# A two-layer transformer block with cross attention on one core: eight PSUM banks divided five and three, one maximum per head

## The chip, the cores and the metric

The kernel runs on one core of a Trainium2 chip. The metric is the device time of one execution in microseconds (us), from runs on the chip. In this kernel TensorE (PE) multiplies and writes to eight PSUM banks (tiles of 128 partitions x 512 fp32 values); VectorE (DVE) and ScalarE (ACT) read them; GpSimd (POOL) works on tiles in SBUF; SyncE (SP) issues most DMAs.

## The reference

The input is x (4 x 512 x 320) and a context (4 x 1601 x 192), fp32. Two layers of the same form follow one another; each adds three parts to x:

```python
h1 = _ln(x, n1_g, n1_b)
x = _attn(h1, h1, q1, k1, v1, o1_w, o1_b, heads) + x        # self attention, 512 keys
h2 = _ln(x, n2_g, n2_b)
x = _attn(h2, context, q2, k2, v2, o2_w, o2_b, heads) + x   # cross attention, 1601 keys
h3 = _ln(x, n3_g, n3_b)
a, g = jnp.split(h3 @ ff_w1 + ff_b1, 2, axis=-1)
x = a * jax.nn.gelu(g, approximate=False) @ ff_w2 + ff_b2 + x
```

Attention has 20 heads of 16 columns and a softmax over all keys.

## The kernel before

**Units and rounds.** Attention is cut into units: one batch and one group of four heads (5 groups), so 20 units of self and 20 of cross attention per layer, then four feed-forward units. main (L1157) runs a unit in rounds, one for each chunk of 128 keys: 4 rounds for self attention, 13 for cross attention, 680 in all. In a round each of the four heads gets its scores (score, L1161): keys on the partitions, 512 queries along the bank, three matmul passes of 32 rows: two for the products of a value split in a high and a low part, and one that subtracts the row maximum (nrows). ACT takes the exponential (L1178). The round after, values (L1185) multiplies the four exponentials with the values (tile av, L1192), ACT copies the result (vo, L1208) and POOL adds it up (L1209).

**Maxima.** The maximum of each query's scores must be known before its unit starts. It is found by computing the scores once more, with queries on the partitions (tile sps, L968), and reducing along the keys on DVE (L985). max_pairs (L945) prepares this work for the unit that is next: for each 128 queries and 512 keys a pair of heads (2, 3) and a pair (0, 1). The 65 keys that are left over in cross attention are done for all queries at once (L996, L1008). give (L1438) hands main one pair of each kind per round, as long as there are some; what is left runs in extra rounds of its own (L1233, L1242), in which start["both"] is set.

**How a round is ordered.** The heads use different rows of the PE array, so passes of different heads run side by side. round_of (L1140) makes all tiles of a round first, lays their passes out in slots by the rows they use, issues slot after slot, and only then issues the readers (exponentials and reductions):

```python
made = [f() for f in products]
...
for at in sorted(slots):
    for p in slots[at]:
        p()
for _, _, then in made:
    then()
```

The products are scores 0 and 1, pair (2, 3), scores 2 and 3, pair (0, 1). So the slots are: scores 0, 1 with maxima 2, 3 (two slots); then scores 2, 3 start where the maxima end, and maxima 0, 1 start in the fourth slot, after scores 0 and 1.

**Side steps.** Between rounds, steps (L429) runs work for later units by costs and due times: projections (qkps, qps, kps), values (vps), the output projection (ops), norms. Queries and keys that have been projected go through DMAs to their places. Each engine executes its instructions in the order in which the program issues them.

**The banks.** Two pools hold the eight PSUM banks. ps_st (L97) has four single banks: scores, av, and the side steps' tiles (step_bank, L369). ps_m (L98) has two tiles of two banks: a pair of maxima, reduced by one DVE instruction, fills one. quarter_banks (L871), for the keys and values of the context (L826, L910), takes two single banks and one pair: ACT copies the singles (L835, L918), DVE the pair with one instruction (L836, L919). The feed-forward part (banks, L1324) takes two single banks and one pair for two chunks. A tile that is allocated waits until the readers of an earlier tile in its bank are done; the wait stands on the first matmul that writes the bank.

Of the kernel before, what the change touches and what calls it, by code (L numbers as in the profile page):

```python
# [9 lines left out]
F32 = mybir.dt.float32  # L10
# [3 lines left out]
ALU = mybir.AluOpType  # L14
AX = mybir.AxisListType
PSUM = bass.MemoryType.PSUM

B, N, D = 4, 512, 320
S2, CTX = 1601, 192
H, DH = 20, 16  # L20
# [3 lines left out]
P = 128  # L24
NQ = N // P
G, HG = 5, 4
# [15 lines left out]
HALF = QT // 2  # L42
# [24 lines left out]
def kernel(ctx: ExitStack, tc: tile.TileContext, x, context, ws, out):  # L67
# [18 lines left out]
    nc = tc.nc  # L86
# [7 lines left out]
    shared = ctx.enter_context(tc.tile_pool(name="shared", bufs=1))  # L94
    prs = ctx.enter_context(tc.tile_pool(name="prs", bufs=9))
    dram = ctx.enter_context(tc.tile_pool(name="dram", bufs=1, space=bass.MemoryType.DRAM))
    ps_st = ctx.enter_context(tc.tile_pool(name="ps_st", bufs=4, space=PSUM))  # L97
    ps_m = ctx.enter_context(tc.tile_pool(name="ps_m", bufs=2, space=PSUM))  # L98
    ctx.enter_context(tc.manual_schedule())


# [267 lines left out]
    def step_bank(shape, name):  # L369

        if start["on"] and start["both"]:
            return ps_m.tile([P, 2, 512], F32, tag="m", name=name)[:, 0]
        return ps_st.tile(shape, F32, tag="st", name=name)

    def warm(n):
# [312 lines left out]
    def add_proj(u):  # L688
# [129 lines left out]
        def keys_of_context():  # L818

            pss, singles, pair = quarter_banks("kps")  # L820
            for k in range(KB):
                for a, ps in enumerate(pss):
                    rows = slice(a * SLOT, (a + 1) * SLOT)
                    for i in range(2):
                        w = HALF + 32
                        nc.tensor.matmul(  # L826
                            ps[i * GD : (i + 1) * GD, :w],
                            lhsT=wk_q[rows, k, u.g * GD : (u.g + 1) * GD],
                            rhs=first.kvT[rows, k, i * HALF : i * HALF + w],
                            start=(k == 0),  # L830
                            stop=(k == KB - 1),
                        )
            low, high = (room[n].rearrange("p (a w) -> p a w", a=4) for n in ("low", "high"))
            for i, ps in enumerate(singles):
                nc.scalar.copy(low[:, 3 * i, :], ps[:, : HALF + 32])  # L835
            nc.vector.tensor_copy(low[:, 1:3, :], pair[:, :, : HALF + 32])  # L836
            split(room["low"], room["high"])

            parts = high, low

            def full(i):
                to = u.kT[:, : 4 * QT].rearrange("p (a w) -> p a w", a=4)
                return [
                    (to[h::2, :, i * HALF : (i + 1) * HALF], t[i * GD : (i + 1) * GD, :, :HALF]) for h, t in enumerate(parts)
                ]

            def ends():
                to = u.kT[:, 4 * QT :].rearrange("p (a w) -> p a w", a=4)
                return [(to[h::2], t[GD:, :, HALF:]) for h, t in enumerate(parts)]

            move("k", lambda: full(0), free, GAP + 1)
            move("k", lambda: full(1), free)
            move("k", ends, free)
            first.made["kv"] += 1
# [15 lines left out]

    def quarter_banks(name):  # L871

        both = ps_m.tile([P, 2, 512], F32, tag="m", name=name)
        singles = [ps_st.tile([P, 512], F32, tag="st", name=name) for _ in range(2)]
        return [singles[0], both[:, 0], both[:, 1], singles[1]], singles, both

    def add_values(u):

# [23 lines left out]
        def values_of_context(i, s):  # L902

            h0, h1 = PARTS[i]
            w = (h1 - h0) * DH
            pss, singles, both = quarter_banks("vps")
            for k in range(KB):
                for a, ps in enumerate(pss):
                    rows = slice(a * SLOT, (a + 1) * SLOT)
                    nc.tensor.matmul(  # L910
                        ps[:, :w],
                        lhsT=u.kvT[rows, k, s * P : (s + 1) * P],
                        rhs=wv_q[rows, k, h0 * DH : h1 * DH],
                        start=(k == 0),
                        stop=(k == KB - 1),
                    )
            for a, ps in enumerate(singles):
                nc.scalar.copy(vals[:, 4 * s + 3 * a, h0:h1, 0:DH], ps[:, :w].rearrange("p (h d) -> p h d", d=DH))  # L918
            nc.vector.tensor_copy(  # L919
                vals[:, 4 * s + 1 : 4 * s + 3, h0:h1, 0:DH],  # L920
                both[:, :, :w].rearrange("p a (h d) -> p a h d", d=DH),
            )
            u.vmade[i] += 4

        for i, g in enumerate((0, 2)):
# [19 lines left out]
    def max_pairs(u):  # L945
# [8 lines left out]
        def banks(heads):  # L954


            if start["both"] and heads[0] == 0:
                pss = [ps_st.tile([P, 512], F32, tag="st", name="sps") for _ in heads]
                return pss, [ps.rearrange("p (o w) -> p o w", o=1) for ps in pss]
            ps = ps_m.tile([P, 2, 512], F32, tag="m", name="sps")  # L960
            return [ps[:, i] for i in range(2)], [ps]

        def full_two(heads, t, s):
            pss, parts = banks(heads)

            def product(e):
                for j, ps in zip(heads, pss):
# [11 lines left out]
                to = u.pm[:, t, :, s]  # L979

            def reduce():
                n = 2 // len(parts)
                for i, part in enumerate(parts):
                    j = heads[0] + i
                    nc.vector.tensor_reduce(to[:, j : j + n], part, AX.X, ALU.max, negate=(ns == 1))  # L985

            return heads, [lambda e=e: product(e) for e in range(2)], reduce

        def rest_two(heads):
            pss, parts = banks(heads)  # L990
            w = rest + rest % 2

            def product(t):
# [8 lines left out]
                        )  # L1002

            def reduce():
                n = 2 // len(parts)
                for i, part in enumerate(parts):
                    j = heads[0] + i
                    nc.vector.tensor_reduce(  # L1008
                        u.pm[:, :, j : j + n, full].rearrange("p t j -> p j t"),
                        part[:, :, : NQ * w].rearrange("p j (t w) -> p j t w", w=w)[:, :, :, :rest],  # L1010
                        AX.X,
                        ALU.max,
                    )

            return heads, [lambda t=t: (product(t), product(t + 1)) for t in range(0, NQ, 2)], reduce
# [141 lines left out]
    def main(u, give, nxt):  # L1157
# [55 lines left out]
        for c in range(u.nch):  # L1213
            extra = []
            if last:

                both = ps_m.tile([P, 2, N], F32, tag="m", name="st")
                round_of([lambda j=j: score(c, j, both[:, j % 2] if j > 1 else None) for j in range(HG)])
                tick()
            else:  # L1220
                products = []
# [48 lines left out]
    def ff_main(u, give, nxt):  # L1270
# [50 lines left out]
            nc.scalar.activation(gl, pss[1], AF.Gelu, bias=b1[:, NHC + c : NHC + c + 1])  # L1321
            nc.vector.scalar_tensor_tensor(hid[c], pss[0], b1[:, c : c + 1], gl, ALU.add, ALU.mult)  # L1322

        def banks():  # L1324
            gates = ps_m.tile([P, 2, 512], F32, tag="m", name="fps")
            return [[ps_st.tile([P, 512], F32, tag="st", name="fps"), gates[:, e]] for e in range(2)]


        pss = None
        for c in range(0, NHC, 2):  # L1330
            ahead = pss is not None
            if not ahead:
                beside(True, 2)
                pss = banks()

            for e in range(2):
                if e or ahead:
# [3 lines left out]
            if not ahead:  # L1341
                rests(c, these, False)
                if c + 2 < NHC:
                    pss = banks()
                    rests(c + 2, pss, True)
            for e in range(2):
                gate(c + e, these[e])
# [221 lines left out]
```

## Time and profile before

| what | value |
| --- | --- |
| median of 3 runs | 3118.38 us (3117.67 to 3122.93) |
| the profiled execution | 3113.44 us, of which its span 3111.7 us |
| granted TensorE clock | 0.993 of full speed |
| attention of layer 0, from 390 us to 1300 us | PE busy 882.18 us of 910.00, DVE 708.91, ACT 711.12 |
| feed-forward of layer 0, from 1300 us to 1590 us | PE busy 287.45 us of 290.00, DVE 77.71, ACT 42.02 |

In the profile, a line number (L968) is a line of the kernel before. A group of instructions shows the tile written and the tiles read, the count, its busy time with the mean of one in ns, and the time that its engine stood idle before it with what ended that. PE shows matmuls, PEld the loading of their weights. A timeline row is the start, the time taken, the engine, the line and the operation. A matmul of fp32 operands leaves two records, one of the split operands one.

### The profile page before, as it was taken

What the parts mean: (1) busy time and instruction counts of PE and PEld (TensorE: products, weight loads), DVE (VectorE), ACT (ScalarE), POOL (GpSimd) and SP (SyncE); (2) the same over time, 40 slices, a digit from 0 to 9 for tenths busy, and PEclk for the clock granted to TensorE, in tenths of its full rate; (3) what the DMA queues carried; (4) which work ended last, traced back from release to release, by engine and by line L of the source; (5) the groups of instructions that cost most, each with busy time, mean ns of one, the idle gap of its engine ahead of it and who ended that gap; (6) DMA issues with size and microseconds to landing.
All of it is one profiled execution on the core that took longest, in us unless ns stands there. A gap on an engine that the chain in (4) does not pass through costs nothing.

```text
span 3111.7 us, 81138 instructions
## 1 busy us (share of the span) xinstructions
PE 2997.5 (96%) x34290; PEld 1601.3 (51%) x34290; DVE 2115.3 (68%) x2834; ACT 1961.0 (63%) x3909; POOL 1129.4 (36%) x1213
## 2 busy tenths in 40 slices
PE   7999899999999999999999998999999999999999
PEld 4555455455455555355555554554545545544555
DVE  5887877877878788522258778778787787774221
ACT  3776567777877778611137765678778778784110
POOL 3434234444444543311114442445444444431000
PEclk8999999999999999999999999999999999999999
DMA  3433122221221221200114332211221122102000
GB/s 96 112 87 104 48 66 62 67 51 40 62 56 36 62 53 27 82 6 0 31 31 105 88 83 53 58 46 45 53 55 41 42 58 47 44 16 80 9 13 13
DMA packets 188189, 165.54 MB, mean 53 GB/s; under 512 B 67748, under 2 KB 152880, under 8 KB 187824
## 3 DMA queue, kind: packets, MB, share of 16 engines
q1 hardware_dynamic: 187240, 159.28, 20.1%
q8 instruction: 270, 4.42, 0.6%
q14 instruction: 95, 0.78, 0.1%
q10 hardware_dynamic: 360, 0.53, 0.1%
q0 software_dynamic: 224, 0.53, 0.1%
HBM read 43.53 MB, written 28.90 MB: 23 GB/s over the span
## 4 chain that ended last, share of the span: by engine, by line
PE 78%; DVE 14%; ACT 5%; issue 1%; POOL 1%; SPq 0%; DMA 0%; ACTq 0%; POOLq 0%; DVEq 0%
PE st L1168 23%; PE av L1192 18%; PE fps L1298 9%; DVE pm L985 6%; PE yps L1352 6%; PE qkps L763 4%; ACT pr L1178 4%; PE kps L826 3%; PE sps L968 3%; PE vps L910 3%; PE ops L1102 3%; PE fps L1311 2%; DVE nmax L985 2%; PE qps L802 2%; PE vps L892 2%
## 5 line engine op out<-in xcount | busy, mean ns | idle before, releaser
L1178 ACT ACTIVATE pr<-st 128x512 f32<-128x512 f32 (+1 forms) x2720 | 1405.4, 603 | 340.7 <-PE st L1168 277.2
L985 DVE TENSOR_REDUCE pm<-sps 128x2 f32<-128x1024 f32 (+1 forms) x982 | 1129.1, 1192 | 124.0 <-PE sps L968 107.0
L1209 POOL TENSOR_TENSOR o<-o,vo 128x512 f32<-128x512 f32 x576 | 741.7, 1288 | 1271.5 <-ACT vo L1208 1265.1
L1168 PE MATMUL st<-q,kT 32*128 32x512 f32 (+1 forms) x5120 | 951.5, 436 | 19.8 <-DVE x L1109 8.2
L968 PE MATMUL sps<-kT,q 32*128 32x512 f32 x4800 | 840.2, 437 | 39.3 <-DVE pm L985 19.5
L1192 PE MATMUL av<-pr,vals 128*32 128x512 f32 (+1 forms) x5440 | 736.8, 608 | 32.3 <-ACT pr L1178 25.5
L1168 PEld LDWEIGHTS st<-q,kT 32*128 32x128 f32 (+1 forms) x5120 | 468.2, 180 | 495.3 <-ACT pr L1178 277.1
L1168 PE MATMUL st<-nrows,ones 32*128 32x512 f32 (+1 forms) x2720 | 631.1, 395 | 0.1
L985 DVE TENSOR_REDUCE nmax<-sps 128x2 f32<-128x1024 f32 (+1 forms) x338 | 377.5, 1160 | 110.0 <-PE sps L968 107.8
L968 PEld LDWEIGHTS sps<-kT,q 32*128 32x128 f32 x4800 | 363.9, 183 | 91.5 <-DVE pm L985 52.4
L1208 ACT COPY vo<-av 128x512 f32<-128x512 f32 x576 | 348.6, 605 | 31.5 <-PE av L1192 23.7
L1168 PEld LDWEIGHTS st<-nrows,ones 32*128 32x128 f32 (+1 forms) x2720 | 329.0, 180 | 32.2 <-issue 0.6
L1321 ACT ACTIVATE gl<-fps,b 128x512 f32<-128x512 f32 x80 | 50.7, 684 | 385.2 <-PE fps L1311 275.4
L1298 PE MATMUL fps<-hT,w 128*128 128x512 f32 x640 | 283.7, 597 | 1.1 <-DVE hid L1322 1.1
L1192 PEld LDWEIGHTS av<-pr,vals 128*32 128x32 f32 (+1 forms) x5440 | 110.7, 108 | 290.4 <-ACT pr L1178 279.9
L1322 DVE SCALAR_TENSOR_TENSOR hid<-fps,b,gl 128x512 f32<-128x512 f32 x80 | 56.4, 746 | 255.2 <-ACT gl L1321 255.2
L1298 PEld LDWEIGHTS fps<-hT,w 128*128 128x128 f32 x640 | 119.2, 190 | 150.8 <-issue 144.9
L1352 PE MATMUL yps<-w,hid 128*128 128x320 f32 x640 | 175.8, 434 | 0.4 <-ACT hT L535 0.4
L1352 PEld LDWEIGHTS yps<-w,hid 128*128 128x128 f32 x640 | 120.5, 190 | 56.0 <-issue 6.6
L1102 PEld LDWEIGHTS ops<-wo,aT 112*32 112x32 f32 (+1 forms) x3072 | 97.4, 110 | 61.3 <-issue 29.7
L763 PE MATMUL qkps<-hT,wqk 112*128 112x256 f32 (+1 forms) x480 | 125.1, 404 | 0.9 <-DVE hid L1322 0.9
L1102 PE MATMUL ops<-wo,aT 112*32 112x160 f32 (+1 forms) x3072 | 124.1, 300 | 0.9 <-DVE pm L985 0.5
(92 smaller groups left out, 2409.8 us busy)
## 6 DMA issues: line engine op xcount, KB each, us to landing
kT<-stages SPq DMA_DIRECT2D x160, 192.0 KB
oway<-o SPq DMA_DIRECT2D x80, 256.0 KB
q<-high SPq DMA_DIRECT2D x160, 64.0 KB
q<-low SPq DMA_DIRECT2D x160, 64.0 KB
kT<-high SPq DMA_DIRECT2D x60, 128.0 KB
q<-low SPq DMA_DIRECT2D x58, 128.0 KB
kT<-low SPq DMA_DIRECT2D x58, 128.0 KB
q<-high SPq DMA_DIRECT2D x56, 128.0 KB
```

The lines of the kernel that those rows point to most:

```text
L763: nc.tensor.matmul(ps[:, :w], lhsT=wqk[:n, k, u.g].rearrange("p i d -> p (i d)"), rhs=first.hT[:n, k, at : at + w], start=(k == 0), stop=( ...
L826: nc.tensor.matmul(ps[i * GD : (i + 1) * GD, :w], lhsT=wk_q[rows, k, u.g * GD : (u.g + 1) * GD], rhs=first.kvT[rows, k, i * HALF : i * HAL ...
L968: nc.tensor.matmul(ps, lhsT=u.q[j * SLOT : (j + 1) * SLOT, e, t * P : (t + 1) * P], rhs=u.kT[j * SLOT : (j + 1) * SLOT, u.k0 + s * 512 : u ...
L985: nc.vector.tensor_reduce(to[:, j : j + n], part, AX.X, ALU.max, negate=(ns == 1))
L1102: nc.tensor.matmul(ps[f : f + m, : D // 2], lhsT=aT[:n, k, t * P + f : t * P + f + m], rhs=wo[:n, k, cols], start=(k == 0), stop=(k == 2),)
L1168: nc.tensor.matmul(st[:r, :], lhsT=ones[rows, :r] if e == 2 else u.keys(rows, c), rhs=u.rows[rows, :] if e == 2 else u.q[rows, e, :], star ...
L1178: nc.scalar.activation(p[:r], st[:r], AF.Exp)
L1192: nc.tensor.matmul(ps[j * SLOT : (j + 1) * SLOT, :], lhsT=columns_of[:r, head : head + SLOT], rhs=pr.pop((c, j))[:r, :], start=True, stop= ...
L1208: nc.scalar.copy(vo, ps)
L1209: nc.gpsimd.tensor_tensor(u.o, u.o, vo, ALU.add)
L1298: nc.tensor.matmul(ps, lhsT=w1[:, k, i * FF + c * P : i * FF + (c + 1) * P], rhs=u.hT[:, k, :], start=ahead and k == 0, stop=not ahead and ...
L1352: nc.tensor.matmul(ps[:, :D], lhsT=hid[c][:, t * P : (t + 1) * P], rhs=w2[:, c, :], start=(c == 0), stop=(c == NHC - 1),)
```

## The change

ps_st gets five banks, and ps_m three single banks instead of two pairs. A pair of maxima takes two tiles of ps_m and is reduced by two DVE instructions, one per head; the pair that DVE copied in the context's keys and values becomes two tiles and two copies. A side step in an extra round takes one bank of ps_m instead of a pair. In the last unit of a layer, scores 2 and 3 take a bank each. The feed-forward part takes two banks of each pool for the first two chunks and, for the two chunks that follow at once, three of ps_st and one of ps_m.

```diff
@@ -94,8 +94,8 @@
     shared = ctx.enter_context(tc.tile_pool(name="shared", bufs=1))
     prs = ctx.enter_context(tc.tile_pool(name="prs", bufs=9))
     dram = ctx.enter_context(tc.tile_pool(name="dram", bufs=1, space=bass.MemoryType.DRAM))
-    ps_st = ctx.enter_context(tc.tile_pool(name="ps_st", bufs=4, space=PSUM))
-    ps_m = ctx.enter_context(tc.tile_pool(name="ps_m", bufs=2, space=PSUM))
+    ps_st = ctx.enter_context(tc.tile_pool(name="ps_st", bufs=5, space=PSUM))
+    ps_m = ctx.enter_context(tc.tile_pool(name="ps_m", bufs=3, space=PSUM))
     ctx.enter_context(tc.manual_schedule())
 
 
@@ -369,7 +369,7 @@
     def step_bank(shape, name):
 
         if start["on"] and start["both"]:
-            return ps_m.tile([P, 2, 512], F32, tag="m", name=name)[:, 0]
+            return ps_m.tile([P, 512], F32, tag="m", name=name)
         return ps_st.tile(shape, F32, tag="st", name=name)
 
     def warm(n):
@@ -833,7 +833,8 @@
             low, high = (room[n].rearrange("p (a w) -> p a w", a=4) for n in ("low", "high"))
             for i, ps in enumerate(singles):
                 nc.scalar.copy(low[:, 3 * i, :], ps[:, : HALF + 32])
-            nc.vector.tensor_copy(low[:, 1:3, :], pair[:, :, : HALF + 32])
+            for i, ps in enumerate(pair):
+                nc.vector.tensor_copy(low[:, 1 + i, :], ps[:, : HALF + 32])
             split(room["low"], room["high"])
 
             parts = high, low
@@ -870,9 +871,8 @@
 
     def quarter_banks(name):
 
-        both = ps_m.tile([P, 2, 512], F32, tag="m", name=name)
-        singles = [ps_st.tile([P, 512], F32, tag="st", name=name) for _ in range(2)]
-        return [singles[0], both[:, 0], both[:, 1], singles[1]], singles, both
+        scored, maxed = ([pool.tile([P, 512], F32, tag=tag, name=name) for _ in range(2)] for pool, tag in ((ps_st, "st"), (ps_m, "m")))
+        return [scored[0], maxed[0], maxed[1], scored[1]], scored, maxed
 
     def add_values(u):
 
@@ -916,10 +916,10 @@
                     )
             for a, ps in enumerate(singles):
                 nc.scalar.copy(vals[:, 4 * s + 3 * a, h0:h1, 0:DH], ps[:, :w].rearrange("p (h d) -> p h d", d=DH))
-            nc.vector.tensor_copy(
-                vals[:, 4 * s + 1 : 4 * s + 3, h0:h1, 0:DH],
-                both[:, :, :w].rearrange("p a (h d) -> p a h d", d=DH),
-            )
+            for a, ps in enumerate(both):
+                nc.vector.tensor_copy(
+                    vals[:, 4 * s + 1 + a, h0:h1, 0:DH], ps[:, :w].rearrange("p (h d) -> p h d", d=DH),
+                )
             u.vmade[i] += 4
 
         for i, g in enumerate((0, 2)):
@@ -954,14 +954,11 @@
         def banks(heads):
 
 
-            if start["both"] and heads[0] == 0:
-                pss = [ps_st.tile([P, 512], F32, tag="st", name="sps") for _ in heads]
-                return pss, [ps.rearrange("p (o w) -> p o w", o=1) for ps in pss]
-            ps = ps_m.tile([P, 2, 512], F32, tag="m", name="sps")
-            return [ps[:, i] for i in range(2)], [ps]
+            pool, tag = (ps_st, "st") if start["both"] and heads[0] == 0 else (ps_m, "m")
+            return [pool.tile([P, 512], F32, tag=tag, name="sps") for _ in heads]
 
         def full_two(heads, t, s):
-            pss, parts = banks(heads)
+            pss = banks(heads)
 
             def product(e):
                 for j, ps in zip(heads, pss):
@@ -979,15 +976,13 @@
                 to = u.pm[:, t, :, s]
 
             def reduce():
-                n = 2 // len(parts)
-                for i, part in enumerate(parts):
-                    j = heads[0] + i
-                    nc.vector.tensor_reduce(to[:, j : j + n], part, AX.X, ALU.max, negate=(ns == 1))
+                for j, ps in zip(heads, pss):
+                    nc.vector.tensor_reduce(to[:, j : j + 1], ps, AX.X, ALU.max, negate=(ns == 1))
 
             return heads, [lambda e=e: product(e) for e in range(2)], reduce
 
         def rest_two(heads):
-            pss, parts = banks(heads)
+            pss = banks(heads)
             w = rest + rest % 2
 
             def product(t):
@@ -1002,14 +997,9 @@
                         )
 
             def reduce():
-                n = 2 // len(parts)
-                for i, part in enumerate(parts):
-                    j = heads[0] + i
+                for j, ps in zip(heads, pss):
                     nc.vector.tensor_reduce(
-                        u.pm[:, :, j : j + n, full].rearrange("p t j -> p j t"),
-                        part[:, :, : NQ * w].rearrange("p j (t w) -> p j t w", w=w)[:, :, :, :rest],
-                        AX.X,
-                        ALU.max,
+                        u.pm[:, :, j, full], ps[:, : NQ * w].rearrange("p (t w) -> p t w", w=w)[:, :, :rest], AX.X, ALU.max,
                     )
 
             return heads, [lambda t=t: (product(t), product(t + 1)) for t in range(0, NQ, 2)], reduce
@@ -1214,8 +1204,9 @@
             extra = []
             if last:
 
-                both = ps_m.tile([P, 2, N], F32, tag="m", name="st")
-                round_of([lambda j=j: score(c, j, both[:, j % 2] if j > 1 else None) for j in range(HG)])
+                round_of([
+                    lambda j=j: score(c, j, ps_m.tile([P, N], F32, tag="m", name="st") if j > 1 else None) for j in range(HG)
+                ])
                 tick()
             else:
                 products = []
@@ -1321,9 +1312,12 @@
             nc.scalar.activation(gl, pss[1], AF.Gelu, bias=b1[:, NHC + c : NHC + c + 1])
             nc.vector.scalar_tensor_tensor(hid[c], pss[0], b1[:, c : c + 1], gl, ALU.add, ALU.mult)
 
-        def banks():
-            gates = ps_m.tile([P, 2, 512], F32, tag="m", name="fps")
-            return [[ps_st.tile([P, 512], F32, tag="st", name="fps"), gates[:, e]] for e in range(2)]
+        def banks(spare):
+            def bank(e):
+                pool, tag = (ps_m, "m") if e else (ps_st, "st")
+                return pool.tile([P, 512], F32, tag=tag, name="fps")
+
+            return [[bank(0), bank(not spare)], [bank(0), bank(1)]]
 
 
         pss = None
@@ -1331,7 +1325,7 @@
             ahead = pss is not None
             if not ahead:
                 beside(True, 2)
-                pss = banks()
+                pss = banks(False)
 
             for e in range(2):
                 if e or ahead:
@@ -1341,7 +1335,7 @@
             if not ahead:
                 rests(c, these, False)
                 if c + 2 < NHC:
-                    pss = banks()
+                    pss = banks(True)
                     rests(c + 2, pss, True)
             for e in range(2):
                 gate(c + e, these[e])
```

## The prediction

> **What bounds the kernel now.** I read the page first: busy shares, then the chain of work that ended last.
>
> ```profile
> span 3111.7 us, 81138 instructions
> PE 2997.5 (96%) x34290; PEld 1601.3 (51%) x34290; DVE 2115.3 (68%) x2834; ACT 1961.0 (63%) x3909; POOL 1129.4 (36%) x1213
> ...
> PE 78%; DVE 14%; ACT 5%; issue 1%; POOL 1%; SPq 0%; DMA 0%; ACTq 0%; POOLq 0%; DVEq 0%
> ```
>
> TensorE (PE) is busy in 96% of the span and holds 78% of the chain. Its queue runs in order, so whatever makes one matmul wait makes all behind it wait. Next, the groups by line, with PE's idle time and its releasers:
>
> ```profile
> L1192 PE MATMUL av<-pr,vals 128*32 128x512 f32 (+1 forms) x5440 | 736.8, 608 | 32.3 <-ACT pr L1178 25.5
> L968 PE MATMUL sps<-kT,q 32*128 32x512 f32 x4800 | 840.2, 437 | 39.3 <-DVE pm L985 19.5 <-DVE nmax L985 12.6 <-DMA q<-high 7.0
> L968 PE MATMUL sps<-kT 32*128 32x512 f32 x320 | 55.8, 425 | 0.1
> L996 PE MATMUL sps<-kT,q 32*128 32x66 f32 x1280 | 79.1, 275 | 1.1 <-DVE pm L985 1.1
> ```
>
> Eight av records make a round, so 5440 are 680 rounds. PE hardly idles before maxima (39.3 us) or av (32.3 us). Where the wait for a bank of maxima ends decides this change, so I read one round in the timeline, one without a side step (start, us taken, engine, line):
>
> ```profile
> 602.17 0.16 PEld L1192 LDWEIGHTS av<-pr,vals 65*32 65x32 f32 x8 [0.36 <-ACT pr L1178]
> 603.17 0.50 PE L1168 MATMUL st<-q,kT 32*128 32x512 f32 x2
> 603.18 0.50 PE L968 MATMUL sps<-kT,q 32*128 32x512 f32 x2
> 603.38 0.62 ACT L1208 COPY vo<-av 128x512 f32<-128x512 f32 x1
> 603.52 0.40 PE L968 MATMUL sps<-kT,q 32*128 32x512 f32 x2
> 603.97 2.36 DVE L985 TENSOR_REDUCE pm<-sps 128x2 f32<-128x1024 f32 x2 [0.36 <-PE sps L968]
> 604.05 0.18 PEld L1168 LDWEIGHTS st<-q,kT 32*128 32x128 f32 x2 [0.30 <-ACT vo L1208]
> 604.06 0.50 PE L968 MATMUL sps<-kT,q 32*128 32x512 f32 x2
> 604.39 0.40 PE L968 MATMUL sps<-kT,q 32*128 32x512 f32 x2
> 604.62 0.39 PE L1168 MATMUL st<-nrows,ones 32*128 32x512 f32 x1
> 604.94 0.16 PEld L1192 LDWEIGHTS av<-pr,vals 128*32 128x32 f32 x8 [0.37 <-ACT pr L1178]
> ```
>
> The round takes 2.77 us from av to av. Heads 2 and 3 get their two score passes for the maximum at 603.18 and 603.52. Their reduction starts at 603.97, 0.80 after the round's first score. But heads 0 and 1 start at 604.06, only 0.09 later, long before that reduction is done. That costs nothing now: they write the other pair of banks. The last pass starts at 604.62, 1.45 into the round, and av at 604.94, 1.77 into it. A round that follows a side step looks the same, without the small wait for vo:
>
> ```profile
> 698.28 0.49 PE L1168 MATMUL st<-q,kT 32*128 32x512 f32 x2
> 699.07 2.36 DVE L985 TENSOR_REDUCE pm<-sps 128x2 f32<-128x1024 f32 x2 [0.58 <-PE sps L968]
> 699.09 0.39 PE L968 MATMUL sps<-kT,q 32*128 32x512 f32 x1
> 699.99 0.16 PEld L1192 LDWEIGHTS av<-pr,vals 128*32 128x32 f32 x8 [0.61 <-ACT pr L1178]
> ```
>
> Reduction 0.79 after the round's start, the second heads at 0.81, av at 1.71.
>
> **The change, part by part.** PE, ACT, POOL and SP execute the same instructions in the same order; only waits move. DVE gets more and smaller reductions and copies.
>
> *Three banks for four heads (the loss).* round_of takes four maxima banks per round (heads 2, 3, 0, 1), and all passes are queued before any reduction. With three banks, head 1 must take the bank of head 2 of its own round: its first pass waits until DVE has reduced head 2. What queues behind it on PE is the rest of the round: head 0's and head 1's second passes, the last pass of scores 2 and 3, av, and the side step. Late after that are the exponentials of heads 2 and 3, which read those scores. The price needs a reduction of a single head, which the trace already has, grouped by shape:
>
> ```profile
> L985 DVE TENSOR_REDUCE pm<-sps 128x2 f32<-128x1024 f32 x938 | 1102.8, 1216 | 124.0 <-PE sps L968 107.0 <-PE st L1168 16.2
> L985 DVE TENSOR_REDUCE nmax<-sps 128x2 f32<-128x1024 f32 x302 | 356.2, 1217 | 107.3 <-PE sps L968 105.1 <-PE st L1168 1.8
> L985 DVE TENSOR_REDUCE pm<-sps 128x1 f32<-128x512 f32 x44 | 28.1, 680 | 0.0
> L985 DVE TENSOR_REDUCE nmax<-sps 128x1 f32<-128x512 f32 x36 | 23.0, 681 | 2.7 <-PE sps L968 2.7
> L836 DVE COPY stages<-kps 128x448 f32<-128x448 f32 x40 | 25.0, 624 | 106.4 <-PE kps L826 104.3 <-POOL o L1209 2.1
> L919 DVE COPY vals<-vps 128x384 f32<-128x384 f32 x24 | 13.4, 558 | 45.2 <-PE vps L910 45.2
> L919 DVE COPY vals<-vps 128x256 f32<-128x256 f32 x24 | 10.1, 422 | 26.5 <-PE vps L910 26.5
> ```
>
> A single head takes 0.68 us. The handover to PE is 0.05: vo ends at 604.00 and the score that waits for it starts at 604.05. Counted from the round's first score, with DVE on time: head 1 may start at 0.80 + 0.68 + 0.05 = 1.53. Its second pass follows 0.33 later, as 604.39 follows 604.06 after a wait, so at 1.86; av follows the last pass by 0.32 (604.62 to 604.94), so at 2.18. Against 1.77 and 1.71 that is 0.41 and 0.47, or **0.44 per round**. The 0.32 could be partly av's old wait for an exponential, which the fifth bank takes away, and the 0.33 could be one ordinary 0.23 step (604.39 to 604.62). I keep both, since they are what the rows show after a wait; without them I take 0.30 as the low end.
>
> DVE isn't always on time. Outside the reductions listed it is busy 2115.3 - 1510.1 = 605.2 us, at most 0.89 per round. In a round without a step the reduction of head 0 starts 0.45 after its second pass (603.52 to 603.97), and that of head 1 follows 0.64 later (28.1 us for 44, since two overlap a little), so the last one ends near 1.86 + 0.45 + 0.64 + 0.68 = 3.63. The next round starts about 1.00 after av (602.17 to 603.17), at 3.18, and its head 2 can be reduced at 3.98: 0.35 is free. 0.89 - 0.35 = 0.54 would be late; a side step (in about half of the rounds, which I estimate) covers it, which leaves 0.27 per round at most. Part of this is in the time already (the two 'DVE' waits on L968), and a longer round gives DVE more room. I take 0.06, near the low end, and keep 0.27 for the range. So **0.50 per round**, between 0.30 and 0.71.
>
> How many rounds: 5120 full passes are 1280 pairs, 1280 short ones 80 pairs (16 matmuls each). The 80 single-head reductions are 40 pairs that ran in extra rounds beside 40 of the ordinary kind, so 1280 - 80 + 80 = 1280 pairs lie in main rounds: 640 rounds. 640 x 0.50 = **320 us**.
>
> *Context keys and values.* These steps take two of the three maxima banks, in 40 + 48 steps. The next round's head 3 then waits, in its very first pass, for the first of two separate copies; now the pair's copy is needed only by heads 0 and 1, late in the round. Two such rounds, keys and values:
>
> ```profile
> 565.44 0.50 PE L1168 MATMUL st<-q,kT 32*128 32x512 f32 x2
> ...
> 565.60 0.62 DVE L836 COPY stages<-kps 128x448 f32<-128x448 f32 x1 [2.66 <-PE kps L826]
> ```
>
> ```profile
> 421.44 0.48 PE L1168 MATMUL st<-q,kT 32*128 32x512 f32 x2
> ...
> 421.88 0.38 DVE L919 COPY vals<-vps 128x256 f32<-128x256 f32 x1
> ```
>
> The copy starts 0.16 and 0.44 into the round. Half a copy I estimate from the table as half its elements plus a fixed part: 0.39 for keys (0.624 less 0.23), about 0.30 for values. Head 3 goes at 0.60 and 0.79 instead of 0; I take 0.55 and 0.70, since a few of these steps have other work behind them: 40 x 0.55 + 48 x 0.70 = **56 us**, between 30 and 75.
>
> *One maximum instruction per head.* 1240 pair reductions become 2480. Two singles cost 1.28 (28.1/44, twice) against 1.18 (1102.8/938): 0.10 x 1240 = 124 us of DVE. DVE is at 68%, and PE's longer rounds hide it; without that cover it is part of the 0.27 above.
>
> *Five score banks (the gain).* Now the fifth allocation of a round, av, takes the bank of the round's first score and waits for its exponential; afterwards it doesn't. Scores 2 and 3 no longer wait for vo (0.30 at 604.05). Both gains lie ahead of or beside the new wait of head 1, so the 0.44 contains what survives. In the feed-forward part two pairs of chunks fill all eight banks, before as after, and what comes next waits for the same gates; I put it at nothing, 10 us either way.
>
> **Sum**: 320 + 56 = 376 us on the profiled execution's 3113.44, so 3489.8; I say **3490**. The median of the runs shown is 3118.38, 0.16% above the profiled one, which is inside the rounding.
>
> **The rivals.**
>
> *DVE becomes the bound.* Every transposition or normalisation ahead of head 2's reduction is paid by PE in full, and the added 124 us too: 0.75 per round, 640 x 0.75 + 56 = 536, so 3650. For it, from the view of this one line, where DVE stood idle before a reduction:
>
> ```profile
> its engine sat idle before it (us, times) until:
>   PE sps L968: 214.8, 334
> ```
>
> 334 of 1320 reductions, where 680 first ones of a round could have, so DVE is often late; and three banks leave no store of work. Against: a round of 3.2 us holds four singles, 2.6 us, with time left.
>
> *The wait is half hidden.* If the passes refill faster than the rows show and the freed av and score waits pay back, some 0.25 per round is left: 160 + 56, so 3330.
>
> *Faster.* One mechanism: head 2's single reduction ends before head 1 wants the bank, so only the fifth bank's gain remains: the 25.5 us before av, the waits for vo, and some 0.1 in about 300 rounds, together near 60 us: 3055. It decides at the point where 0.80 + 0.73 falls below the 0.81 to 0.89 at which head 1 starts; that takes an order in which head 2's passes run 0.7 earlier. The Trainium skill, Perfetto Trace Analysis, section "Optimizing Scalar/DVE Operations", speaks for this side: where the vector engine isn't saturated but makes others wait, smaller instructions can get results out sooner. By that rule, with 68% here, the result would be this gain; the trace agrees that 0.68 comes sooner than 1.22, but the pair's 1.22 isn't waited for in its own round today.
>
> *The change does nothing*: the scheduler could reuse banks so that no wait falls in the same round; then 3113. The allocation order speaks against it.
>
> **How the numbers follow.** Forecast 0.60 (its own range 3420 to 3560), DVE as the bound 0.20, half hidden 0.14, faster 0.04, nothing 0.02. The ends of the unknown costs are 640 x 0.30 + 30 = 222 and 640 x 0.71 + 75 + 10 = 539, so 3335 to 3653. Range: **3340 to 3650**, which leaves out about half of the DVE rival, half of the half-hidden one and the last two, some 0.2. About 0.2% is what a measurement here can tell from no change: faster 0.04, within 0.02, slower 0.94.
>
> **What would show it.** In the profile after: a PE wait on DVE of about 0.7 us before a sps matmul in nearly every round, against 39.3 us in all now; rounds without a step near 3.2 us; av no longer waiting for ACT; x2560 single reductions of 0.68. A wait of st or sps on the copies in 88 rounds shows the second term. I am wrong if idle time before sps stays under 100 us, or if reductions run behind one another without a pause (then DVE is the bound).

## The result and the profile after

The changed kernel takes 3472.14 us (median of 4 runs, 3470.61 to 3485.12), the kernel before 3119.55 in the same session: a ratio of 1.1144, 95% interval 1.1124 to 1.1164. It is 353 us slower. The profiled execution took 3472.2 us against 3113.44, 359 more. I said 3490, with a range from 3340 to 3650.

The page of the changed kernel, with the same rows as before the prediction:

```profile
span 3470.4 us, 82567 instructions
PE 3183.3 (92%) x34290; PEld 1602.4 (46%) x34290; DVE 2241.4 (65%) x4240; ACT 2072.4 (60%) x3909; POOL 1122.3 (32%) x1213
...
PE 73%; DVE 22%; issue 2%; ACT 1%; POOL 1%; SPq 0%; DMA 0%; ACTq 0%; POOLq 0%; DVEq 0%
```

PE executes the same 34290 matmuls. DVE went from 14% to 22% of the chain, although it isn't fuller (65% of the span against 68%): PE now waits for it, not because DVE has too much to do, but because of when it does it. The groups by line, with the idle time and its releasers:

```profile
L1182 PE MATMUL av<-pr,vals 128*32 128x512 f32 (+1 forms) x5440 | 744.9, 619 | 0.0
L965 PE MATMUL sps<-kT,q 32*128 32x512 f32 x4800 | 1118.2, 451 | 256.5 <-DVE pm L980 177.5
L965 PEld LDWEIGHTS sps<-kT,q 32*128 32x128 f32 x4800 | 471.3, 186 | 564.9 <-DVE pm L980 391.9
L980 DVE TENSOR_REDUCE pm<-sps 128x1 f32<-128x512 f32 x1920 | 1231.0, 684 | 255.3 <-PE sps L965 221.7
L1158 PE MATMUL st<-q,kT 32*128 32x512 f32 (+1 forms) x5120 | 840.5, 429 | 5.9 <-ACT pr L1168 2.2
```

PE idles 256.5 us ahead of maxima, 39.3 before; av's 32.3 are gone, as the fifth bank promised. The timeline shows the round that was read for the prediction; here it starts at 667.01:

```profile
667.01 0.50 PE L1158 MATMUL st<-q,kT 32*128 32x512 f32 x2
667.35 0.40 PE L965 MATMUL sps<-kT,q 32*128 32x512 f32 x2
667.79 2.04 DVE L980 TENSOR_REDUCE pm<-sps 128x1 f32<-128x512 f32 x3 [0.53 <-PE sps L965]
667.81 0.39 PE L965 MATMUL sps<-kT,q 32*128 32x512 f32 x1
667.81 0.40 PE L1158 MATMUL st<-q,kT 32*128 32x512 f32 x2
668.53 0.49 PE L965 MATMUL sps<-kT,q 32*128 32x512 f32 x1 [0.32 <-DVE pm L980]
668.54 0.70 PE L965 MATMUL sps<-kT,q 32*128 32x512 f32 x2
669.17 0.16 PEld L1182 LDWEIGHTS av<-pr,vals 128*32 128x32 f32 x8 [0.35 <-ACT pr L1168]
```

Head 0 still starts at 0.80 (667.81), but head 1 only at 1.52 (668.53), 0.05 after the first of the reductions that began at 667.79 is over. av follows at 2.16, against 1.77. The idle column says 0.32 for this wait, though head 1 comes 0.72 after head 0. The records of head 0's pass and of the scores reach 0.40 into the wait, so PE counts as busy in that time. So PE's busy time grew by 186 us with the same matmuls (the lower clock, below, adds to it), and its idle time alone would show only half of the loss.

I also compared the two traces round by round, from one av's first matmul to the next, 679 intervals in the same order:

| rounds with one pair of each kind | count | longer by, mean us | median us |
| --- | --- | --- | --- |
| without a side step | 313 | 0.48 | 0.46 |
| with another side step | 220 | 0.48 | 0.51 |
| with the context's keys | 35 | 1.13 | 0.95 |
| with the context's values | 46 | 1.05 | 0.97 |

These four rows alone are 151 + 106 + 39 + 48 = 344 us.

Some of this goes with the clock, whose mean is 0.983 against 0.993. In the traces the granted clock stands at full rate or, for short stretches, at half rate. Here are three windows of the changed kernel, the first with a wait of PE of 2.03 us in it; the clock is the third number from the end, 1.00 or 0.51:

```profile
core 0: us, PE busy (x) PEld busy (x) DVE busy (x) ACT busy (x) POOL busy (x), PEclk, DMA share, GB/s
601.10:604.50 3.40, 1.37 (x20) 0.69 (x13) 3.30 (x10) 1.57 (x3) 1.27 (x1) 1.00 0.40 116
604.50:607.90 3.40, 3.40 (x25) 1.36 (x23) 2.08 (x5) 1.67 (x3) 0.39 (x1) 0.51 0.03 5
607.90:611.30 3.40, 3.17 (x29) 1.45 (x25) 3.22 (x7) 2.90 (x6) 1.01 (x2) 0.99 0.02 5
```

The changed kernel is at half rate for 116.0 us in 23 stretches, the kernel before for 45.4 us in 9. Of the 533 rounds in the first two rows of the table, 504 are at full rate in both traces; these are longer by 0.43 us in the mean.

### The profile page after: what moved, and what is told of

Its sections match the earlier page's. It is cut to its first block, busy times and chain, and to the rows that moved or that the text cites. A ratio compares the mean times of both kernels' runs of the same rounds, so it can differ in the third digit from the quotient of the medians.

```text
span 3470.4 us, 82567 instructions
## 1 busy us (share of the span) xinstructions
PE 3183.3 (92%) x34290; PEld 1602.4 (46%) x34290; DVE 2241.4 (65%) x4240; ACT 2072.4 (60%) x3909; POOL 1122.3 (32%) x1213
## 4 chain that ended last, share of the span: by engine, by line
PE 73%; DVE 22%; issue 2%; ACT 1%; POOL 1%; SPq 0%; DMA 0%; ACTq 0%; POOLq 0%; DVEq 0%
PE av L1182 16%; PE sps L965 14%; DVE pm L980 13%; PE st L1158 11%; PE fps L1289 8%; PE yps L1346 5%; DVE nmax L980 4%; PE qkps L763 3%; PE ops L1092 3%; PE vps L910 3%; PE kps L826 3%; PE fps L1302 2%; PE vps L892 2%; PE qps L802 2%; PE sps L991 1%
## 5 line engine op out<-in xcount | busy, mean ns | idle before, releaser
L1168 ACT ACTIVATE pr<-st 128x512 f32<-128x512 f32 (+1 forms) x2720 | 1460.3, 595 | 445.2 <-PE st L1158 346.5
L980 DVE TENSOR_REDUCE pm<-sps 128x1 f32<-128x512 f32 x1920 | 1231.0, 684 | 255.3 <-PE sps L965 221.7
L965 PE MATMUL sps<-kT,q 32*128 32x512 f32 x4800 | 1118.2, 451 | 256.5 <-DVE pm L980 177.5
L1158 PE MATMUL st<-q,kT 32*128 32x512 f32 (+1 forms) x5120 | 840.5, 429 | 5.9 <-ACT pr L1168 2.2
L965 PEld LDWEIGHTS sps<-kT,q 32*128 32x128 f32 x4800 | 471.3, 186 | 564.9 <-DVE pm L980 391.9
L1158 PEld LDWEIGHTS st<-q,kT 32*128 32x128 f32 (+1 forms) x5120 | 438.0, 183 | 403.1 <-ACT pr L1168 277.4
L1158 PE MATMUL st<-nrows,ones 32*128 32x512 f32 (+1 forms) x2720 | 603.4, 444 | 0.0
L980 DVE TENSOR_REDUCE nmax<-sps 128x1 f32<-128x512 f32 x640 | 409.6, 685 | 152.3 <-PE sps L965 134.7
L1198 ACT COPY vo<-av 128x512 f32<-128x512 f32 x576 | 337.9, 587 | 161.0 <-PE av L1182 159.5
L1158 PEld LDWEIGHTS st<-nrows,ones 32*128 32x128 f32 (+1 forms) x2720 | 251.8, 182 | 21.2
```

Of the source, the lines that this page charges most:

```text
L965: nc.tensor.matmul(ps, lhsT=u.q[j * SLOT : (j + 1) * SLOT, e, t * P : (t + 1) * P], rhs=u.kT[j * SLOT : (j + 1) * SLOT, u.k0 + s * 512 : u ...
L980: nc.vector.tensor_reduce(to[:, j : j + 1], ps, AX.X, ALU.max, negate=(ns == 1))
L1158: nc.tensor.matmul(st[:r, :], lhsT=ones[rows, :r] if e == 2 else u.keys(rows, c), rhs=u.rows[rows, :] if e == 2 else u.q[rows, e, :], star ...
L1168: nc.scalar.activation(p[:r], st[:r], AF.Exp)
L1198: nc.scalar.copy(vo, ps)
```

## The experiments

Each stands against the kernel before, which ran beside it, with a median of 3118 to 3120 us in each session. The theory is that of the prediction: head 1 waits, in its own round, for head 2's reduction, since three banks serve four heads. The rivals: DVE's smaller instructions and its load; and the division of the banks itself.

### e1_split_only

One maximum instruction per head in the kernel before, with its pairs of banks:

```diff
-                n = 2 // len(parts)
-                for i, part in enumerate(parts):
-                    j = heads[0] + i
-                    nc.vector.tensor_reduce(to[:, j : j + n], part, AX.X, ALU.max, negate=(ns == 1))
+                for j, ps in zip(heads, pss):
+                    nc.vector.tensor_reduce(to[:, j : j + 1], ps, AX.X, ALU.max, negate=(ns == 1))
...
```

> The kernel before with its four single banks and two pairs, but one maximum instruction per head. Bank theory (the loss is head 1 waiting, in its own round, for the reduction of head 2, because only three banks serve four heads): that wait isn't here, the 124 us that DVE works longer hide behind PE; 3115 to 3160 us. Rival (the smaller and more numerous DVE instructions are the loss, DVE falls behind): near 3470, at least 3300.

Measured: 3149.83 us, ratio 1.0106 (1.009 to 1.0123), so 32 us slower. The groups by line:

```profile
L983 DVE TENSOR_REDUCE pm<-sps 128x1 f32<-128x512 f32 x1920 | 1184.4, 681 | 99.9 <-PE sps L968 80.8 <-PE st L1161 15.3
L968 PE MATMUL sps<-kT,q 32*128 32x512 f32 x4800 | 843.5, 440 | 46.1 <-DVE pm L983 23.1 <-DVE nmax L983 14.7 <-DMA q<-high 7.3
```

The reductions are as many and as long as in the changed kernel, and PE idles 46.1 us ahead of maxima, not 256.5. So splitting is not the loss. But it isn't free: the median round is unchanged, and 30 us lie in 33 rounds that are over 0.2 us longer. In the 658 rounds at full clock rate in both traces the split costs 22 us.

### e2_four_four

```diff
-    ps_st = ctx.enter_context(tc.tile_pool(name="ps_st", bufs=5, space=PSUM))
-    ps_m = ctx.enter_context(tc.tile_pool(name="ps_m", bufs=3, space=PSUM))
+    ps_st = ctx.enter_context(tc.tile_pool(name="ps_st", bufs=4, space=PSUM))
+    ps_m = ctx.enter_context(tc.tile_pool(name="ps_m", bufs=4, space=PSUM))
...
-                    pss = banks(True)
+                    pss = banks(False)
```

> The changed kernel with the banks divided four and four instead of five and three (the feed-forward part takes two of each for every two chunks). Bank theory: the fourth maxima bank takes the wait away; 3115 to 3160 us, as for the kernel before with split reductions. Rival (smaller DVE instructions and separate copies are the loss): near 3470. If the fifth score bank had given something that the wait covers, this stays above before by nothing of it, and only a kernel with five and four could show it.

Measured: 3155.5 us, ratio 1.0119 (1.0104 to 1.0134). Everything of the change is there but the division of the banks, in attention and in the feed-forward part, and 317 of its 353 us are gone. It is 6 us above e1, which the intervals don't tell apart.

### e3_head2_half and e4_head1_half

The same saving on DVE, once for the head that is waited for and once for another:

```diff
-                    nc.vector.tensor_reduce(to[:, j : j + 1], ps, AX.X, ALU.max, negate=(ns == 1))
+                    nc.vector.tensor_reduce(to[:, j : j + 1], ps[:, : 256 if j == 2 else 512], AX.X, ALU.max, negate=(ns == 1))
```

and with j == 1. Each kernel leaves out half of that head's maximum.

> The changed kernel, where the reduction of head 2 reads 256 of its 512 keys (half of that head's maximum is left out). Its duration should fall from 0.68 to some 0.41 us, 0.27 less. Bank theory: head 1 starts 0.27 earlier in each of some 640 rounds, up to 170 us; 3300 to 3350 us. Rival (DVE as the bound): the same gain as from shortening any other head's reduction.

> The changed kernel, where the reduction of head 1 reads 256 of its 512 keys (half of that head's maximum is left out): the same DVE time is taken away as where head 2's is halved. Bank theory: nothing in the round waits for it, so 0 to 50 us less than the changed kernel, 3420 to 3475 us, by DVE being on time a little more often. Rival (DVE as the bound): as much as with head 2, 3300 to 3350 us.

Measured: 3295.21 us with head 2 halved (ratio 1.0568, 1.0547 to 1.0589), 3449.34 with head 1 halved (1.1062, 1.104 to 1.1085). Taken from 3472.14, that is 177 us against 23. The groups of DVE by line and shape, head 2 halved:

```profile
L980 DVE TENSOR_REDUCE pm<-sps 128x1 f32<-128x256 f32 x480 | 200.2, 417 | 217.2 <-PE sps L965 213.4 <-PE st L1158 2.4
```

The groups by line of the same kernel, and after it of the one with head 1 halved:

```profile
L965 PE MATMUL sps<-kT,q 32*128 32x512 f32 x4800 | 1112.2, 449 | 120.2 <-DVE pm L980 56.8 <-DVE nmax L980 20.5 <-DVE vals L920 10.0
```

```profile
L965 PE MATMUL sps<-kT,q 32*128 32x512 f32 x4800 | 1118.9, 452 | 234.6 <-DVE pm L980 160.7 <-DVE nmax L980 47.6 <-DVE vals L920 10.0
```

A reduction of head 2 that is 0.267 us shorter (0.417 against 0.684) in 640 rounds is 171 us; the kernel gained 177. Head 1's reduction, shortened by as much, gave an eighth of that. Round by round the median is 0.267 us shorter with head 2 halved, and 0.001 us with head 1 halved. DVE as the bound would make the two equal: it falls. Part of the 177 us goes with the clock, 0.988 against 0.983; by the price of half rate found under e10 it is some 15 us, an estimate. The 23 us that head 1 gives fit DVE being late now and then.

### e5_four_three

Four score banks instead of five; the eighth bank serves the feed-forward part alone.

```diff
-    ps_st = ctx.enter_context(tc.tile_pool(name="ps_st", bufs=5, space=PSUM))
+    ps_st = ctx.enter_context(tc.tile_pool(name="ps_st", bufs=4, space=PSUM))
...
+    ps_x = ctx.enter_context(tc.tile_pool(name="ps_x", bufs=1, space=PSUM))
...
-            return [[bank(0), bank(not spare)], [bank(0), bank(1)]]
+            other = ps_x.tile([P, 512], F32, tag="x", name="fps") if spare else bank(1)
+            return [[bank(0), other], [bank(0), bank(1)]]
```

> The changed kernel with four score banks instead of five, three maxima banks as they are (the eighth bank serves the feed-forward part alone). It prices the fifth score bank. Bank theory: av's wait for the round's first exponential and the wait of score 3 for vo come back, but both end before head 1 gets its bank (1.53 us into the round), so nothing is lost: 3465 to 3490 us. Rival (the fifth bank gives a gain of its own, hidden in the sum): 3500 or more.

Measured: 3498.25 us (two runs, 3495.28 and 3501.21), ratio 1.1215 (1.1193 to 1.1238): 26 us over the changed kernel, a miss. The typical round is unchanged (median difference 0.00 us, as the theory has it); the difference lies in some 50 rounds. But the granted clock was lower too, 0.976 against 0.983, and 0.7% of 3499 us is 24. The traces show some of both: the 618 rounds at full rate in both kernels make up 9 us of it, and the 61 in which one of the two is at half rate make up 17 us. e10 and e11 were made to tell the two apart.

### e6_context_banks

```diff
-        scored, maxed = ([pool.tile([P, 512], F32, tag=tag, name=name) for _ in range(2)] for pool, tag in ((ps_st, "st"), (ps_m, "m")))
+        scored, maxed = ([pool.tile([P, 512], F32, tag=tag, name=name) for pool, tag in two] for two in (((ps_st, "st"), (ps_st, "st")), ((ps_m, "m"), (ps_st, "st"))))
```

> The changed kernel, but the steps for the context's keys and values take three score banks and one maxima bank instead of two and two, so that the next round's heads 2 and 3 get banks of the maxima of the round before and don't wait for these steps' copies. Second term of the prediction (head 3 waits for the copy in 88 rounds, 56 us): 3410 to 3430 us. Rival (these rounds lose as much as any other and the copies cost nothing): 3465 to 3475.

Measured: 3463.43 us (3454.96 to 3472.94), ratio 1.1105 (1.1077 to 1.1132): 9 us less, where 40 to 60 were expected. Round by round the term is there: against the changed kernel the 40 rounds after keys are 0.31 us shorter and the 48 after values 0.37, together 12 + 18 = 30 us. 14 of it came back in the rounds without such a step, in a profile with a clock of 0.980 against 0.983. Why the rest of these rounds' surplus stays I didn't settle; scores 2 and 3 now take banks that these steps have just used.

### e7_one_pool

```diff
-    ps_st = ctx.enter_context(tc.tile_pool(name="ps_st", bufs=5, space=PSUM))
-    ps_m = ctx.enter_context(tc.tile_pool(name="ps_m", bufs=3, space=PSUM))
+    ps_st = ctx.enter_context(tc.tile_pool(name="ps_st", bufs=8, space=PSUM))
+    ps_m = ps_st
```

with the one tag for all tiles.

> The changed kernel with one pool of eight single banks for everything, in the order of allocation. Head 1 then takes av's bank (free when vo is copied, about when head 1 starts), and av takes the bank of head 2, which was reduced at 1.5 us of its 1.8 in the round if DVE is on time. Bank theory: 3130 to 3180 us, the price of the split reductions and of late reductions before av. Rival (single banks and single reductions cost it): 3400 or more.

Measured: 3099.3 us (3098.54 to 3100.04), ratio 0.9936 (0.9921 to 0.9951): 20 us faster than the kernel before, with the same split reductions. I had expected 3130 or more. The groups by line:

```profile
L965 PE MATMUL sps<-kT,q 32*128 32x512 f32 x4800 | 924.0, 439 | 22.1 <-DVE nmax L980 7.7 <-DMA q<-high 7.3 <-DVE x L1099 2.5
L1158 PE MATMUL st<-q,kT 32*128 32x512 f32 (+1 forms) x5120 | 809.3, 426 | 2.8 <-DVE pm L980 1.6 <-DVE nmax L980 0.2
L1182 PE MATMUL av<-pr,vals 128*32 128x512 f32 (+1 forms) x5440 | 743.6, 611 | 126.9 <-DVE pm L980 101.5 <-DVE nmax L980 10.1 <-DVE pm L1001 0.7
```

av does wait for head 2's reduction, as expected (126.9 us, 32.3 before). But the median round without a step is 0.07 us shorter than before, and with a step 0.12. Scores no longer wait for vo nor av for an exponential; I take that for the reason, but no run tests it alone. I had priced only the loss.

### e8_six_and_pair

Six single banks, and one pair that heads 2 and 3 of the main rounds share, with one instruction:

```diff
-    ps_st = ctx.enter_context(tc.tile_pool(name="ps_st", bufs=5, space=PSUM))
-    ps_m = ctx.enter_context(tc.tile_pool(name="ps_m", bufs=3, space=PSUM))
+    ps_st = ctx.enter_context(tc.tile_pool(name="ps_st", bufs=6, space=PSUM))
+    ps_m = ctx.enter_context(tc.tile_pool(name="ps_m", bufs=1, space=PSUM))
...
+            if start["both"] or heads[0] == 0:
+                return [ps_st.tile([P, 512], F32, tag="st", name="sps") for _ in heads], None
+            ps = ps_m.tile([P, 2, 512], F32, tag="m", name="sps")
+            return [ps[:, i] for i in range(2)], ps
```

> Six single banks for scores, values, steps and heads 0 and 1, and one pair for heads 2 and 3 with one instruction. No bank is taken again in its own round except av's (first score). Against the kernel before, half of the reductions are split and score 3 no longer waits for vo (some 0.1 us in 313 rounds). Bank theory: 3090 to 3140 us, a little under the kernel before if the wait for vo counts; the rival (split reductions cost in themselves) 3135 or more.

Measured: 3125.63 us (6 runs, 3122.28 to 3134.18), ratio 1.0026 (1.0013 to 1.0039). In the range, but not under the kernel before.

### e9_head1_score_bank

Five and three as in the change, but head 1's bank comes from the five:

```diff
-            return [pool.tile([P, 512], F32, tag=tag, name="sps") for _ in heads]
+            pools = [(ps_st, "st") if j == 1 else (pool, tag) for j in heads]
+            return [pool.tile([P, 512], F32, tag=tag, name="sps") for pool, tag in pools]
```

> The changed kernel, five and three as it is, but head 1 takes its bank from the score banks. The three maxima banks then serve three heads, and head 1's bank is that of the result that ACT copies, free when it starts. Bank theory: the wait of head 1 for head 2 is gone and with it nearly all of the loss; the split reductions' 30 us and some waits of scores stay: 3120 to 3165 us. Rival (five and three or the small copies lose something by themselves): 3200 or more.

Measured: 3165.42 us (3161.9 to 3169.92), ratio 1.0155 (1.0138 to 1.0171). The groups by line:

```profile
L966 PE MATMUL sps<-kT,q 32*128 32x512 f32 x4800 | 939.0, 437 | 48.7 <-DVE vals L920 13.0 <-DVE x L1100 10.3 <-DVE nmax L981 7.4
```

One allocation moved, and 307 of the 353 us are gone; of the 256.5 us that PE idled ahead of maxima 48.7 are left. Most of what stays over the kernel before is seen round by round: 0.48 and 0.51 us in the 35 + 46 rounds after context keys and values, 40 us in all. That is the second term of the prediction, here by itself.

### e10_filled_wait and e11_filled_four_three

The first pass of scores 2 and 3 is repeated twice, where PE would soon wait; in the changed kernel, and in that of e5:

```diff
+            def opening():
+                for _ in range(fill):
+                    product(0, True)
+                product(0)
...
+                    fill = 2 if odd and pair else 0
```

> The changed kernel, where the first pass of scores 2 and 3 is issued three times in rounds with maxima (each repeat starts anew, the result is the same): 0.45 us more work for PE, in the time in which it waits for head 1's bank (from 1.26 to 1.53 us into a round if DVE is on time, longer if not). It asks whether the lower granted clock of the changed kernel (0.983 against 0.99) comes from that idling. Bank theory with the clock: PE idles less, the clock goes to 0.988 or more, 3440 to 3475 us in spite of the added work. Bank theory alone: the clock stays, and the added passes fit in the wait but for some 0.2 us in rounds on time: 3475 to 3600.

> The same filling in the kernel with four score banks and three maxima banks. Against the filled kernel with five it prices the fifth score bank with the clock more alike: if the 26 us between the kernels with four and five came from the clock, the two filled ones agree within 10 us; if they are the fifth bank's own, 20 us or more remain.

Measured: 3457.36 us (3456.11 to 3458.28), ratio 1.1091 (1.1072 to 1.1109), and 3487.32 us (3484.52 to 3490.91), ratio 1.1187 (1.117 to 1.1204). The mean granted clock of the changed kernel and of the filled one, and PE's wait ahead of maxima in the filled one:

```profile
core 0: 3470.4 us, clock 0.983
```

```profile
core 0: 3455.0 us, clock 0.989
```

```profile
L965 PE MATMUL sps<-kT,q 32*128 32x512 f32 x4800 | 1121.8, 451 | 77.5 <-DVE pm L980 36.7 <-DVE nmax L980 17.6 <-DVE vals L920 10.0
```

With 2552 more matmuls (36842 against 34290) the kernel is 15 us faster. The wait hides the added work: idle time ahead of maxima falls from 256.5 to 77.5 us. And the clock is higher by 0.006: 79.0 us at half rate in 18 stretches, against 116.0 in 23.

Round by round, the clock is the whole of this gain. The 637 rounds at full rate in both traces differ by 0.2 us taken together. In 14 rounds the changed kernel alone is at half rate, for 37 us; these are 14 us longer in it than in the filled kernel. So 1 us at half rate costs some 0.38 us, and the 71 us that the changed kernel has over the kernel before are worth some 27 of the 353 us: an estimate from these two traces.

The two filled kernels still lie 30 us apart, at 0.986 and 0.989. The 640 rounds at full rate in both make up 21 us of it, where the pair without filling (e5 and the changed kernel) had 9. So the fifth bank has a worth of its own, some 10 to 20 us by these traces, and the rest goes with the clock; my expectation for e5, that nothing is lost, was wrong on that.

## Why the prediction was right

- **The reading.** PE was the bound and in order, and the place to look was the bank that head 1 takes. That held: the wait's removal (e2, e9) takes away 307 to 317 us, and halving one head's reduction moves the typical round by just what was taken from it (e3), another head's hardly (e4).
- **The price of a round.** Head 1 was to start at 1.53 and av at 2.18; the medians of the 313 rounds without a step are 1.53 and 2.19. The 0.44 of an on-time round was 0.46 without a step and 0.51 with one, and the 0.50 with late reductions was 0.48 in the mean. But the 0.06 for late reductions came out near by luck. In the 504 rounds at full clock rate the mean is 0.43, just the on-time price, and 0.44 in the 513 such rounds of the filled kernel. What lifts the mean of all 533 to 0.48 is the rounds at half rate, and the clock isn't in the prediction. DVE is late at times (e4), but it was before, too: av came 1.94 us into a round without a step in the mean, against 1.81 in the median.
- **Keys and values.** The surplus over other rounds is 1.13 - 0.48 = 0.65 in 35 rounds and 1.05 - 0.48 = 0.57 in 46, so 23 + 26 = 49 us; I had 56. e6 took 30 us of it away; what makes the rest is open. The timeline of the changed kernel after a step for keys:

```profile
442.13 0.50 PE L1158 MATMUL st<-q,kT 32*128 32x512 f32 x2
...
442.29 0.69 DVE L837 COPY stages<-kps 128x224 f32<-128x224 f32 x2 [7.67 <-PE kps L826]
442.73 0.18 PEld L965 LDWEIGHTS sps<-kT,q 32*128 32x128 f32 x1 [0.42 <-DVE stages L837]
...
444.09 0.49 PE L965 MATMUL sps<-kT,q 32*128 32x512 f32 x1 [0.15 <-DVE pm L980]
```

  The weights of head 3 load 0.60 into the round, the number of the prediction; head 1 waits once more at 444.09. The copies take 386 ns for keys and 353 or 286 for values, where I estimated 0.39 and 0.30.
- **One instruction per head.** I hid the added 124 us of DVE behind PE's longer rounds. In e1, whose typical round isn't longer, the split costs 32 us. In the changed kernel the rounds at full rate show nothing beyond the on-time price, so the cover fits; no run tests it by itself.
- **The fifth bank.** I let the 0.44 hold what survives of its gain. The typical round agrees; but e5 and e11 show some 10 to 20 us of its own in rare rounds that I hadn't seen. They are inside the 353, on the side of the gain.
- **The feed-forward part**, put at nothing within 10 us: from its first matmul to its last it took 301.0 and 277.2 us before, 297.2 and 275.7 after.
- **What I left out**: the clock, 0.993 to 0.983, some 27 us by the estimate under e10. With it the sum reads 640 x 0.44 = 282 for the wait, 49 for keys and values and 27 for the clock, 358 against the 359 by which the profiled executions differ; that it closes so well is in part chance, since the 27 is an estimate. I had 282, 56 and, for lateness, 38: the mechanism and the two main terms held, and the lateness stood in the clock's place. (The prediction's last addition, 3113.44 + 376, gives 3489.44 and not 3489.8, which the rounding to 3490 covers.)
- **What I said would show it.** av's waits vanished, reductions of 0.68 came 2560 strong, idle time before sps passed 100 us. Rounds without a step took 3.2 us in the median, as I named. But I looked for 0.7 us of idle PE per round, and the column has half of it; the rest is in records that overlap the wait.

Of the rivals, DVE as the bound fell with e4, the half-hidden wait with e3. The faster side had its rule of smaller instructions for results sooner: e1 shows the smaller instructions alone as 1% slower, and e7 shows them in a kernel that is 0.6% faster, once the banks are free for everyone. That gain comes from the banks' order, which the rule doesn't speak of.

## What to carry to other kernels

Count the tiles of a pool that one group of work holds before its first reader is issued; with one bank less, the group waits for itself in every repetition, however idle the reader is on average. Here a reader of 0.68 us cost 0.43 us per round: head 1 starts later, but av then follows it after 0.66 us instead of 0.88. What was taken from the reader came back in full (e3). Price such a wait from the timeline of one repetition: the reader's start, its duration at the new size, and the moment of the first write that needs the bank. A common pool can serve short-lived tiles better than a fixed division (here 0.9936 of the time before, e7), so try it ahead of moving a bank from one division to the other.

## What the runs showed of the hardware

The granted TensorE clock swings between full and half rate, and a change of the waits moves it: 45.4 us at half rate before, 116.0 in the changed kernel, 79.0 where its waits are filled with repeats. What starts a stretch is not settled. It is hardly the ordinary short wait: of PE's 606 waits ahead of maxima that are over 0.15 us, the median is 0.33 us, but 15 of the 23 stretches begin within 7 us after the end of a wait of PE of over 1 us, of which the changed kernel has 33 and the filled one 19. On the other hand e7 has 56 such waits and 14 stretches with 65.8 us, and e5 has 27 such waits and 29 stretches with 170.7 us.

The Trainium skill, TensorE: Matmul & The Clock Gate, section "A second HAM failure mode: psum-queue depth-cycling", tells of a kernel in which frequent short pauses between groups of matmuls, while banks are cycled, let the clock swing between half and full rate. The trace agrees on the swing; in size it is 1% of the clock here, and that the short pauses are its cause is not shown.
